# An edge layer on Trainium2: pair terms in four quarters of m times 32 channels

## The chip, the cores and the metric

One program runs on one core of one Trainium2 chip. The metric is the device time of an execution in microseconds. Three runs of the kernel before took 3580.55, 3586.84 and 3589.28 us; the median is 3586.84. Engines are named as in the profile: PE multiplies matrices (PEld loads its weights), DVE, ACT and POOL work elementwise, SP issues transfers. PSUM is the memory that PE writes its sums to, in eight banks of 512 f32 per partition; SBUF is the working memory.

## The reference

The input x is 4 samples of 56 x 56 pixels x 128 channels. Four layers follow one another, each with a group normalisation ahead and a residual sum behind. The change touches layer 1, the edge layer. In each sample and row l it forms, for every pair of pixels (n, m) of the row, a term of 128 channels, and sums over m:

```python
W1, W2 = (We[:, :f], We[:, f:])
proj_i = jnp.einsum('blnf,of->blno', x, W1)
proj_j = jnp.einsum('blnf,of->blno', x, W2)
edge = jax.nn.relu(proj_i[:, :, :, None, :] + proj_j[:, :, None, :, :] + be)
edge_sum = edge.sum(axis=3)
node_in = jnp.concatenate([x, edge_sum], axis=-1)
node = jax.nn.relu(jnp.einsum('blnc,oc->blno', node_in, Wn) + bn)
```

That is 4 x 56 x 56 x 56 x 128 pair terms. Layer 0 is a windowed attention with a global attention and an MLP, layer 2 a Fourier neural operator with attention over heads, layer 3 a convolution with sums.

## The kernel before

A sample lies as 128 channels (partitions) x 3136 pixels. For each of four samples, `first_layers` runs the attention (`fast_layer`) and then `edge_layer`; layer 2 and 3 follow for all samples. The change is in `edge_layer` (lines 1150 to 1256), `edge_weights` (1259) and the packing of weights in `l1_host` (1268). PE, ACT and DVE run the order of the program text there (a manual schedule); POOL has its own queue in program order.

The layer works in seven blocks of 8 image rows: 8 x 56 = 448 pixels, `NB`. For a block, `project` (line 1180) makes pc = W2 x and pa = W1 x in PSUM, one bank each. `evacuate` (1189) makes on ACT c = -(pc + be) in SBUF, a = pa as a copy in SBUF, and adds the bias bn to the residual. The relu of a pair term, relu(a - c), is max(a, c) - c, and it is made in two ways. A turn is four values of m, and EDGE_TURNS = "ddpddpdpddpddp" says who makes its tile of 128 channels x (4 m x 8 rows x 56 n) = 128 x 1792:

- nine turns "d": DVE writes max(pa, c) (line 1231, tile e_td, seven buffers). It reads pa straight from PSUM, and c from SBUF;
- five turns "p": POOL writes a - c from SBUF (1233, e_tp, four buffers), and ACT takes the relu in place (1235).

PE then sums the tile (1238): sixteen products per turn, each of a 32 x 32 identity with 32 channels x 448, for every pair of m (q) and channel quarter (r). Product (q, r) adds into partitions 32q to 32q + 31 of bank r of `acc`. So the four banks hold, for each quarter of channels, four partial sums over m. `acc` has one buffer of four banks; `mm` (pc, po and others) and `pa` have two banks each. These are all eight.

The max terms lack the sum of c over the m of the "d" turns. DVE makes it once a block (`rest`, line 1248). At the end of a block ACT copies all of acc, 128 x 1792, to SBUF (`e_sums`, 1250), and `output` (1200) forms po = Wn_x x - Wn_e rest + four products that add the quarters up, for the block before; then `project` is issued for the block two ahead. `finish` (1209) on DVE writes max(po, -bn) + (residual + bn), for the block two behind, after turn g = 3. `evacuate(j + 1)` stands after turn 5, the normalisation of block j + 2 after turn 8.

A product of f32 is two records in the profile. A name such as e_td is the tile, without its buffer's number.

Of the kernel before, what the change touches and what calls it, by code (L numbers as in the profile page):

```python
# [12 lines left out]
F32 = mybir.dt.float32  # L13
AF = mybir.ActivationFunctionType
ALU = mybir.AluOpType
AX = mybir.AxisListType
# [3 lines left out]
P = 128  # L20
B = 4
HH = 56
TOK = HH * HH
NB = 448
# [8 lines left out]
def bc(ap, axis, n):  # L33

    ap = ap.unsqueeze(axis)
    shape = list(ap.shape)
    shape[axis] = n
    return ap.to_broadcast(shape)


def blk(j):
    return slice(j * NB, (j + 1) * NB)
# [149 lines left out]
def apply_norm(k, out, xt, mr):  # L192
    k.nc.vector.tensor_scalar(out, xt, mr[:, 0:1], mr[:, 1:2], ALU.subtract, ALU.mult)
# [953 lines left out]
EDGE_TURNS = "ddpddpdpddpddp"  # L1147


def edge_layer(k, w, x1, st):  # L1150

    nc, tc = k.nc, k.tc
    xf = x1.rearrange("p l n -> p (l n)")
    nd = 4 * EDGE_TURNS.count("d")
    quarters = [slice(32 * q, 32 * q + 32) for q in range(4)]
    with ExitStack() as es:  # L1160
        big = es.enter_context(tc.tile_pool(name="e_big", bufs=1))
        wk = es.enter_context(tc.tile_pool(name="e_wk", bufs=2))
        psum = es.enter_context(tc.tile_pool(name="e_ps", bufs=2, space=PSUM))

        def bank():
            return psum.tile([P, 512], F32, tag="mm", name="e_mm")

        mr = group_norm_factors(k, wk, bank, st)
        xg = big.tile([P, TOK], F32, name="e_xg")
        shift = wk.tile([P, 1], F32, name="e_shift", bufs=1)  # L1170
        nc.vector.tensor_scalar(shift, mr[:, 0:1], mr[:, 1:2], -1.0, ALU.mult, ALU.mult)
        ready = {}

        def normed(j):
            if j < 2:
                apply_norm(k, xg[:, blk(j)], xf[:, blk(j)], mr)
            elif j < NBLK:
                nc.scalar.activation(xg[:, blk(j)], xf[:, blk(j)], AF.Identity, bias=shift, scale=mr[:, 1:2])

        def project(j):  # L1180
            if j >= NBLK:
                return
            pc = psum.tile([P, 512], F32, tag="mm", name="e_pc")
            nc.tensor.matmul(pc[:, :NB], w.W2, xg[:, blk(j)], start=True, stop=True)
            pa = psum.tile([P, 512], F32, tag="pa", name="e_pa")
            nc.tensor.matmul(pa[:, :NB], w.W1, xg[:, blk(j)], start=True, stop=True)
            ready[j] = pa, pc

        def evacuate(j):
            if j >= NBLK:  # L1190
                return
            pa, pc = ready[j]
            c = wk.tile([P, 8, HH], F32, name="e_c")
            nc.scalar.activation(c.rearrange("p l m -> p (l m)"), pc[:, :NB], AF.Identity, bias=w.nbe, scale=-1.0)
            a = wk.tile([P, NB], F32, name="e_a")
            nc.scalar.copy(a, pa[:, :NB])  # L1196
            nc.scalar.activation(xf[:, blk(j)], xf[:, blk(j)], AF.Identity, bias=w.bn)
            ready[j] = pa, a, c

        def output(j, rest, sums):  # L1200
            po = psum.tile([P, 512], F32, tag="mm", name="e_po")
            nc.tensor.matmul(po[:, :NB], w.Wn[:, 0, :], xg[:, blk(j)], start=True, stop=False)
            nc.tensor.matmul(po[:, :NB].rearrange("p (l n) -> p l n", l=8), w.nWn, bc(rest, 2, HH),
                             start=False, stop=False)
            for r in range(4):
                nc.tensor.matmul(po[:, :NB], w.Wnq[:, r, :], sums[:, r, :], start=False, stop=(r == 3))  # L1206
            return po

        def finish(j, po):

            nc.vector.scalar_tensor_tensor(xf[:, blk(j)], po[:, :NB], w.nbn, xf[:, blk(j)], ALU.max, ALU.add)

        with tc.manual_schedule(engines={mybir.EngineType.PE, mybir.EngineType.Activation, mybir.EngineType.DVE}):
            for j in range(2):
                normed(j)
            for j in range(2):
                project(j)
                evacuate(j)
            last = po = None
            for j in range(NBLK):  # L1220
                pa, a, c = ready.pop(j)
                acc = psum.tile([P, 4, 512], F32, name="e_acc", bufs=1)
                rest = wk.tile([P, 8], F32, name="e_rest")
                at = {"d": 0, "p": nd}
                for g, e in enumerate(EDGE_TURNS):
                    t = wk.tile([P, 4, 8, HH], F32, tag="e_" + e, name="e_t" + e, bufs=7 if e == "d" else 4)
                    cm = bc(c[:, :, at[e]:at[e] + 4].rearrange("p l m -> p m l"), 3, HH)
                    at[e] += 4
                    if e == "d":
                        am = bc(pa[:, :NB].rearrange("p (l n) -> p l n", l=8), 1, 4)  # L1230
                        nc.vector.tensor_tensor(t, am, cm, ALU.max)  # L1231
                    else:
                        nc.gpsimd.tensor_sub(t, bc(a.rearrange("p (l n) -> p l n", l=8), 1, 4), cm)  # L1233
                        tf = t.rearrange("p m l n -> p (m l n)")
                        nc.scalar.activation(tf, tf, AF.Relu)  # L1235
                    for q in range(4):
                        for r, o in enumerate(quarters):
                            nc.tensor.matmul(acc[quarters[q], r, :NB], k.ident[o, o],  # L1238
                                             t[o, q].rearrange("p l n -> p (l n)"),
                                             start=(g == 0), stop=(g == len(EDGE_TURNS) - 1))  # L1240
                    if g == 3 and po is not None:
                        finish(j - 2, po)
                    if g == 5 and j:
                        evacuate(j + 1)
                    if g == 8:
                        normed(j + 2)
                    if g == 9:
                        nc.vector.tensor_reduce(rest, c[:, :, 0:nd], AX.X, ALU.add)
                sums = wk.tile([P, 4, NB], F32, name="e_sums")
                nc.scalar.copy(sums, acc[:, :, :NB])  # L1250
                if last:
                    po = output(*last)
                project(j + 2)
                last = j, rest, sums
            finish(NBLK - 2, po)
            finish(NBLK - 1, output(*last))


def edge_weights(k, w, pool):

    for n, t in (("nbe", w.be), ("nbn", w.bn), ("nWn", w.Wn[:, 1, :])):
        r = pool.tile(list(t.shape), F32, name="e_" + n)
        k.nc.vector.tensor_scalar_mul(r, t, -1.0)
        setattr(w, n, r)


def l1_host(i):
    We, Wn = i["L1_conv_We"], i["L1_conv_Wn"]
    W2 = Wn[:, P:].T.reshape(4, 1, 32, P)
    return {  # L1270
        "w1_W1": We[:, :P].T, "w1_W2": We[:, P:].T, "w1_be": i["L1_conv_be"].reshape(P, 1),
        "w1_Wn": Wn.T.reshape(2, P, P).transpose(1, 0, 2), "w1_bn": i["L1_conv_bn"].reshape(P, 1),
        "w1_Wnq": np.broadcast_to(W2, (4, 4, 32, P)).reshape(4, P, P).transpose(1, 0, 2),
    }


# [1388 lines left out]
def group_norm_factors(k, pool, bank, st):  # L2665

    nc = k.nc
    mv = pool.tile([P, 2], F32, tag="mv", name="gf_mv")
    nc.vector.bn_aggr(mv, st.rearrange("p a b -> p (a b)"))
    ps = bank()  # L2670
    nc.tensor.matmul(ps[:, 0:1], k.g4, mv[:, 0:1], start=True, stop=True)
    mr = pool.tile([P, 2], F32, tag="mr", name="gf_mr")
    nc.vector.tensor_copy(mr[:, 0:1], ps[:, 0:1])
    t = pool.tile([P, 1], F32, tag="gt", name="gf_t")
    nc.vector.tensor_sub(t, mv[:, 0:1], mr[:, 0:1])
    nc.vector.tensor_mul(t, t, t)
    nc.vector.tensor_add(t, t, mv[:, 1:2])
    ps = bank()
    nc.tensor.matmul(ps[:, 0:1], k.g4, t, start=True, stop=True)
    nc.scalar.activation(t, ps[:, 0:1], AF.Sqrt, bias=k.eps)  # L2680
    nc.vector.reciprocal(mr[:, 1:2], t)
    return mr
# [158 lines left out]
```

## Time and profile before

| what | us |
|---|---|
| median of three runs | 3586.84 |
| the profiled execution, its own time | 3579.81 |
| its span in the profile | 3578.0 |
| PE busy in the span | 3372.0 (94%) |
| DVE busy | 2702.3 (76%) |
| ACT busy | 2089.9 (58%) |
| POOL busy | 1249.2 (35%) |
| first edge layer, 549.2 to 699.7: PE busy | 141.79 |
| the same: DVE, POOL, ACT busy | 130.02, 113.45, 83.44 |

The last two rows are the busy times of the engines in one stretch, and the other three edge layers (1211.3 to 1361.9, 1873.6 to 2024.9, 2540.2 to 2690.9) give nearly the same: DVE 130.1, 129.9 and 129.9, POOL 113.5, 113.5 and 113.7. Durations in the profile are from one execution. A group of instructions is written as line, engine, operation, output <- inputs, shapes, count; then the busy time and the mean nanoseconds of one; then the idle time of the engine just ahead of them and who ended it. PE's busy time says little by itself, since its matmuls overlap; the chain of waits says more.

### The profile page before, as it was taken

The numbers are of one execution on the slowest core, as the hardware profiler recorded it, in microseconds if no ns is written. First come the engines' busy times: TensorE is split into PE (matmuls) and PEld (weight loads), VectorE is DVE, ScalarE is ACT, GpSimd is POOL, SyncE is SP. The second block draws the span as 40 slices with busy tenths as digits, with TensorE's granted clock in tenths as the row PEclk, the third lists the DMA queues.
The fourth block names the chain that finished last, engine by engine and source line by source line (L and its number), as shares of the span: only waits on it lengthen the run. The fifth ranks groups of instructions, "written<-read, shape, count | busy, mean of one in ns | idle before, by whom it ended". The sixth has DMA issues, their size and how long they took to land.

```text
span 3578.0 us, 80873 instructions
## 1 busy us (share of the span) xinstructions
PE 3372.0 (94%) x36096; PEld 1549.4 (43%) x36096; DVE 2702.3 (76%) x2531; ACT 2089.9 (58%) x2103; POOL 1249.2 (35%) x752
## 2 busy tenths in 40 slices
PE   6999998989999898999999999999898899999998
PEld 4433344553333455333344643333456443336664
DVE  6588868767888696688859758887784678886776
ACT  4688865458888564688856458887552112214442
POOL 1000017600000581000018400000673778884686
PEclk8999999999999999999999999999998999999999
DMA  2144420014333000444310024442103027763101
GB/s 103 43 92 92 95 42 20 20 47 94 88 88 83 20 3 20 99 93 94 89 44 3 20 57 94 94 94 63 38 3 101 15 53 178 181 148 91 55 19 55
DMA packets 98076, 244.51 MB, mean 68 GB/s; under 512 B 64456, under 2 KB 69832, under 8 KB 92712
## 3 DMA queue, kind: packets, MB, share of 16 engines
q0 software_dynamic: 16128, 102.77, 14.2%
q1 hardware_dynamic: 74872, 123.64, 11.9%
q10 hardware_dynamic: 6720, 12.85, 1.3%
q8 instruction: 285, 4.67, 0.5%
q14 instruction: 71, 0.58, 0.1%
HBM read 79.46 MB, written 31.33 MB: 31 GB/s over the span
## 4 chain that ended last, share of the span: by engine, by line
PE 79%; DVE 10%; ACT 4%; issue 4%; POOL 3%; DMA 0%; POOLq 0%; DVEq 0%; ACTq 0%
PE f_pm L818 17%; PE f_pm L684 15%; PE u_po L1878 8%; PE e_acc L1238 7%; PE q_acc L1732 3%; DVE e_td L1231 3%; PE f_pm L791 2%; PE e_po L1206 2%; PE f_pm L770 2%; ACT f_ring L821 1%; PE f_pm L464 1%; PE o_d L2141 1%; DVE f_acc L673 1%; PE o_d L2538 1%; PE f_pm L715 1%
## 5 line engine op out<-in xcount | busy, mean ns | idle before, releaser
L821 ACT ACTIVATE f_ring<-f_pm 128x1792 f32<-128x1792 f32 (+1 forms) x764 | 1093.8, 1482 | 228.7 <-PE f_pm L818 181.2
L673 DVE TENSOR_TENSOR f_acc<-f_acc,f_ring 128x1792 f32<-128x1792 f32 x468 | 947.7, 2025 | 191.1 <-ACT f_ring L821 160.9
L818 PE MATMUL f_pm<-f_qT,f_kT 32*128 32x448 f32 x5376 | 725.2, 571 | 15.5 <-ACT f_ring L821 5.1
L684 PE MATMUL f_pm<-f_ring,f_va 128*32 128x448 f32 (+1 forms) x6304 | 589.4, 490 | 0.0
L663 POOL DMA_DIRECT2D f_far<-f_ring x112 | 96.6, 862 | 1329.3 <-ACT f_ring L821 1108.2
L1231 DVE TENSOR_TENSOR e_td<-e_pa,e_c 128x1792 f32<-128x1792 f32 x252 | 491.2, 2018 | 14.1 <-ACT e_a L1196 14.1
L1233 POOL TENSOR_TENSOR e_tp<-e_a,e_c 128x1792 f32<-128x1792 f32 x140 | 451.5, 3261 | 101.4 <-PE e_acc L1238 59.8
L818 PEld LDWEIGHTS f_pm<-f_qT,f_kT 32*128 32x128 f32 x5376 | 260.4, 183 | 417.2 <-ACT f_ring L821 304.7
L1238 PE MATMUL e_acc<-e_td,t_shared 32*32 32x448 f32 x8064 | 325.8, 545 | 24.9 <-DVE e_td L1231 24.0
L684 PEld LDWEIGHTS f_pm<-f_ring,f_va 128*32 128x32 f32 x6304 | 164.2, 109 | 409.7 <-issue 397.4
L1873 DVE TENSOR_TENSOR u_ud<-u_px,u_d 112x1792 f32<-112x1792 f32 x144 | 263.5, 1864 | 39.6 <-PE u_po L1878 35.4
L1235 ACT ACTIVATE e_tp<-e_tp 128x1792 f32<-128x1792 f32 x140 | 233.4, 1694 | 74.0 <-POOL e_tp L1233 74.0
L1875 POOL TENSOR_TENSOR u_up<-xh,u_d 112x1792 f32<-112x1792 f32 (+1 forms) x72 | 240.9, 3376 | 55.0 <-PE u_po L1878 39.7
L1238 PE MATMUL e_acc<-e_tp,t_shared 32*32 32x448 f32 x4480 | 222.6, 544 | 3.0 <-ACT e_tp L1235 2.4
L1878 PE MATMUL u_po<-u_ud,AT 112*64 112x448 f32 x1056 | 213.8, 544 | 1.9 <-DVE u_ud L1873 1.9
L1238 PEld LDWEIGHTS e_acc<-e_td,t_shared 32*32 32x32 f32 x8064 | 142.3, 103 | 138.4 <-DVE e_td L1231 79.4
L1878 PEld LDWEIGHTS u_po<-u_ud,AT 112*64 112x64 f32 x1056 | 74.4, 138 | 128.8 <-issue 112.9
L1250 ACT COPY e_sums<-e_acc 128x1792 f32<-128x1792 f32 x28 | 46.3, 1652 | 136.2 <-PE e_acc L1238 136.2
L1238 PEld LDWEIGHTS e_acc<-e_tp,t_shared 32*32 32x32 f32 x4480 | 96.5, 103 | 53.0 <-issue 16.6
L728 DVE RECIPROCAL f_den<-f_den 128x448 f32<-128x448 f32 x28 | 82.6, 2951 | 44.1 <-ACT f_den L725 44.1
L1717 POOL TENSOR_TENSOR q_u<-iS,q_g 128x1792 f32<-128x1792 f32 x32 | 102.8, 3236 | 23.0 <-PE q_acc L1732 22.8
L1732 PE MATMUL q_acc<-q_u,S 64*64 64x448 f32 x1024 | 104.6, 553 | 4.4 <-DVE q_u L1719 3.3
(525 smaller groups left out, 4511.6 us busy)
## 6 DMA issues: line engine op xcount, KB each, us to landing
f_far<-f_ring POOLq DMA_DIRECT2D x112, 896.0 KB, 6.3
u_d<-dd SPq DMA_DIRECT2D x46, 784.0 KB
f_far<-f_ring SPq DMA_DIRECT2D x28, 896.0 KB
xw<-in_x SPq DMA_DIRECT2D x4, 1568.0 KB
x2d<-x SPq DMA_DIRECT2D x4, 1568.0 KB
xat<-x SPq DMA_DIRECT2D x4, 1568.0 KB
x_xs<-xat ACTq DMA_DIRECT2D x32, 196.0 KB
xm<-x_ev ACTq DMA_DIRECT2D x64, 98.0 KB
```

Of the source, the lines that this page charges most:

```text
L673: nc.vector.tensor_add(e.acc, e.acc, slots(j, c))
L684: nc.tensor.matmul(e.po[heads[h], part], va[o, c, heads[h]], p, start=(c == 0), stop=(c == 23 and part.stop == NB))
L818: nc.tensor.matmul(ss[:, i, :NB], kT[heads[h], c * P:(c + 1) * P], qT[heads[h], blk(j)], start=True, stop=True)
L821: nc.scalar.activation(ring[:, slot:slot + m, :], ss[:, :m, :NB], AF.Exp, scale=scale)
L1231: nc.vector.tensor_tensor(t, am, cm, ALU.max)
L1233: nc.gpsimd.tensor_sub(t, bc(a.rearrange("p (l n) -> p l n", l=8), 1, 4), cm)
L1235: nc.scalar.activation(tf, tf, AF.Relu)
L1238: nc.tensor.matmul(acc[quarters[q], r, :NB], k.ident[o, o], t[o, q].rearrange("p l n -> p (l n)"), start=(g == 0), stop=(g == len(EDGE_TUR ...
L1732: nc.tensor.matmul(acc[bp][i][halves[hb % 2], hb // 2, :NB], x[o], u[o, 8 * hb:8 * hb + 8, :].rearrange("p h t -> p (h t)"), start=first, ...
L1873: nc.vector.tensor_mul(u, bc(px[:, :, :NB], 2, m), dm)
L1875: nc.gpsimd.tensor_mul(u, bc(x, 2, m), dm)
L1878: nc.tensor.matmul(po[64 * b2:64 * b2 + 64, :NB], st.AT[:, 8 * i + h0 + q, 2 * bp + b2, :], u[:, b2, q, :], start=(left == 16), stop=(left ...
```

## The change

The partitions of a pair term's tile are no longer 128 channels. They are four quarters of m times 32 channels, and a tile's first free dimension r is the quarter of the channels. A turn is still a tile of 128 x 1792 elements: one m of each quarter of 56 (M = 14 values a quarter, so 14 turns), for all four r.

- `project` makes pc in sixteen small products (128 x 32 weights, 112 columns), so that partitions 32q hold the m of quarter q; and pa in four products whose weights repeat 32 channels four times, into four banks (pa has one buffer of four banks).
- `evacuate` has two parts, after turns 5 and 7: c = -pc, and a in four pieces of 448 with the bias be. It is now a, in SBUF, that holds be.
- DVE's max and POOL's subtraction both read a and c from SBUF (`terms`).
- PE sums a turn with four products of 128 rows x 32 columns (S, four identities under one another), each into its 32 partitions of one bank. `acc` is one bank with two buffers. The sums of c are four more such products with -S.
- ACT's copy of the sums is 128 x 448, and `output` is two products in place of six.
- In the first block of a sample, the first two DVE tiles are made in pieces of 448, quarter by quarter. Turns of a kind "s" are provided for and don't occur in EDGE_TURNS, which is unchanged.
- `edge_weights` loses two of its three small instructions; `l1_host` packs the weights anew.

```diff
-    nd = 4 * EDGE_TURNS.count("d")
+    M = HH // 4
+    nd, ns = EDGE_TURNS.count("d"), EDGE_TURNS.count("s")
...
-            nc.tensor.matmul(pc[:, :NB], w.W2, xg[:, blk(j)], start=True, stop=True)
-            pa = psum.tile([P, 512], F32, tag="pa", name="e_pa")
-            nc.tensor.matmul(pa[:, :NB], w.W1, xg[:, blk(j)], start=True, stop=True)
-            ready[j] = pa, pc
+            xm = xg[:, blk(j)].rearrange("p (l m) -> p l m", l=8)
+            for r, o in enumerate(quarters):
+                for q in range(4):
+                    nc.tensor.matmul(pc[quarters[q], 8 * M * r:8 * M * (r + 1)].rearrange("p (l m) -> p l m", l=8),
+                                     w.W2[:, o], xm[:, :, M * q:M * (q + 1)], start=True, stop=True)
+            pa = psum.tile([P, 4, 512], F32, name="e_pa", bufs=1)
+            for r in range(4):
+                nc.tensor.matmul(pa[:, r, :NB], w.W1[:, r, :], xg[:, blk(j)], start=True, stop=True)
+            c = wk.tile([P, 4, 8, M], F32, name="e_c")
+            a = wk.tile([P, 4, NB], F32, name="e_a")
+            ready[j] = pc, pa, c, a
...
+            if part == 0:
+                nc.scalar.activation(c.rearrange("p r l m -> p (r l m)"), pc[:, :NB], AF.Identity, scale=-1.0)
+            for r in range(2 * part, 2 * part + 2):
+                nc.scalar.activation(a[:, r, :], pa[:, r, :NB], AF.Identity, bias=w.be[:, r:r + 1])
+            if part == 1:
+                nc.scalar.activation(xf[:, blk(j)], xf[:, blk(j)], AF.Identity, bias=w.bn)
+
+        def terms(j, m, t, r0, r1, e):
+            _, _, c, a = ready[j]
+            cm = bc(c[:, r0:r1, :, m], 3, HH)
+            am = a[:, r0:r1, :].rearrange("p r (l n) -> p r l n", l=8)
+            if e == "d":
+                nc.vector.tensor_tensor(t, am, cm, ALU.max)
+            else:
+                nc.gpsimd.tensor_sub(t, am, cm)
+                tf = t.rearrange("p r l n -> p (r l n)")
+                nc.scalar.activation(tf, tf, AF.Relu)
...
-            nc.tensor.matmul(po[:, :NB].rearrange("p (l n) -> p l n", l=8), w.nWn, bc(rest, 2, HH),
-                             start=False, stop=False)
-            for r in range(4):
-                nc.tensor.matmul(po[:, :NB], w.Wnq[:, r, :], sums[:, r, :], start=False, stop=(r == 3))
+            nc.tensor.matmul(po[:, :NB], w.Wn[:, 1, :], sums, start=False, stop=True)
...
-                acc = psum.tile([P, 4, 512], F32, name="e_acc", bufs=1)
-                rest = wk.tile([P, 8], F32, name="e_rest")
+                acc = psum.tile([P, 512], F32, name="e_acc")
+                rest = wk.tile([P, 4, 8], F32, name="e_rest")
...
+                early = {g: tile_of("d") for g in range(2)} if j == 0 else {}
+                for r in range(4 if early else 0):
+                    for g, t in early.items():
+                        terms(j, at["d"] + g, t[:, r:r + 1], r, r + 1, "d")
...
-                    if e == "d":
-                        am = bc(pa[:, :NB].rearrange("p (l n) -> p l n", l=8), 1, 4)
-                        nc.vector.tensor_tensor(t, am, cm, ALU.max)
...
-                        nc.gpsimd.tensor_sub(t, bc(a.rearrange("p (l n) -> p l n", l=8), 1, 4), cm)
...
-                    for q in range(4):
-                        for r, o in enumerate(quarters):
-                            nc.tensor.matmul(acc[quarters[q], r, :NB], k.ident[o, o],
-                                             t[o, q].rearrange("p l n -> p (l n)"),
-                                             start=(g == 0), stop=(g == len(EDGE_TURNS) - 1))
+                    for t, r0 in parts:
+                        for r in range(t.shape[1]):
+                            nc.tensor.matmul(acc[quarters[r0 + r], :NB], w.S[:, 0, :], t[:, r].rearrange("p l n -> p (l n)"),
+                                             start=(g == 0), stop=False)
...
-                    if g == 5 and j:
-                        evacuate(j + 1)
+                    if g == 5:
+                        evacuate(j + 1, 0)
+                    if g == 7:
+                        evacuate(j + 1, 1)
...
+                for r in range(4):
+                    nc.tensor.matmul(acc[quarters[r], :NB].rearrange("p (l n) -> p l n", l=8), w.S[:, 1, :],
+                                     bc(rest[:, r, :], 2, HH), start=False, stop=True)
+                sums = wk.tile([P, NB], F32, name="e_sums")
+                nc.scalar.copy(sums, acc[:, :NB])
...
+    W1 = np.broadcast_to(We[:, :P].T.reshape(P, 4, 1, 32), (P, 4, 4, 32)).reshape(P, 4, P)
+    S = np.tile(np.eye(32, dtype=np.float32), (4, 1))
```

More of the change, by code (lines that the diff above doesn't have):

```diff
@@ L1183, in project @@
             pc = psum.tile([P, 512], F32, tag="mm", name="e_pc")
-            nc.tensor.matmul(pc[:, :NB], w.W2, xg[:, blk(j)], start=True, stop=True)
-            pa = psum.tile([P, 512], F32, tag="pa", name="e_pa")
-            nc.tensor.matmul(pa[:, :NB], w.W1, xg[:, blk(j)], start=True, stop=True)
-            ready[j] = pa, pc
-        def evacuate(j):
+            xm = xg[:, blk(j)].rearrange("p (l m) -> p l m", l=8)
[3 more added lines that the diff above has]
+                                     w.W2[:, o], xm[:, :, M * q:M * (q + 1)], start=True, stop=True)
@@ L1190, in evacuate @@
+            pa = psum.tile([P, 4, 512], F32, name="e_pa", bufs=1)
[4 more added lines that the diff above has]
+            ready[j] = pc, pa, c, a
+        def evacuate(j, part):
             if j >= NBLK:
                 return
-            pa, pc = ready[j]
-            c = wk.tile([P, 8, HH], F32, name="e_c")
@@ L1194, in evacuate @@
[L1194 to L1200, printed above, removed]
+            pc, pa, c, a = ready[j]
+            if part == 0:
+                nc.scalar.activation(c.rearrange("p r l m -> p (r l m)"), pc[:, :NB], AF.Identity, scale=-1.0)
@@ L1201, in output, with tile_of @@
+        def tile_of(e, n=4):
+            return wk.tile([P, n, 8, HH], F32, tag="e_%s%d" % (e, n), name="e_t" + e,
+                           bufs=2 if n < 4 else 7 if e == "d" else 4)
+        def output(j, sums):
             po = psum.tile([P, 512], F32, tag="mm", name="e_po")
             nc.tensor.matmul(po[:, :NB], w.Wn[:, 0, :], xg[:, blk(j)], start=True, stop=False)
-            nc.tensor.matmul(po[:, :NB].rearrange("p (l n) -> p l n", l=8), w.nWn, bc(rest, 2, HH),
-                             start=False, stop=False)
@@ L1215, in edge_layer @@
                 normed(j)
-            for j in range(2):
-                project(j)
-                evacuate(j)
+            project(0)
+            for part in range(2):
+                evacuate(0, part)
+            project(1)
             last = po = None
             for j in range(NBLK):
-                pa, a, c = ready.pop(j)
-                acc = psum.tile([P, 4, 512], F32, name="e_acc", bufs=1)
-                rest = wk.tile([P, 8], F32, name="e_rest")
-                at = {"d": 0, "p": nd}
-                for g, e in enumerate(EDGE_TURNS):
-                    t = wk.tile([P, 4, 8, HH], F32, tag="e_" + e, name="e_t" + e, bufs=7 if e == "d" else 4)
-                    cm = bc(c[:, :, at[e]:at[e] + 4].rearrange("p l m -> p m l"), 3, HH)
-                    at[e] += 4
-                    if e == "d":
-                        am = bc(pa[:, :NB].rearrange("p (l n) -> p l n", l=8), 1, 4)
-                        nc.vector.tensor_tensor(t, am, cm, ALU.max)
-                    else:
-                        nc.gpsimd.tensor_sub(t, bc(a.rearrange("p (l n) -> p l n", l=8), 1, 4), cm)
-                        tf = t.rearrange("p m l n -> p (m l n)")
-                        nc.scalar.activation(tf, tf, AF.Relu)
-                    for q in range(4):
-                        for r, o in enumerate(quarters):
-                            nc.tensor.matmul(acc[quarters[q], r, :NB], k.ident[o, o],
-                                             t[o, q].rearrange("p l n -> p (l n)"),
-                                             start=(g == 0), stop=(g == len(EDGE_TURNS) - 1))
@@ new lines, in edge_layer @@
+                acc = psum.tile([P, 512], F32, name="e_acc")
+                rest = wk.tile([P, 4, 8], F32, name="e_rest")
+                at = {"d": 0, "p": nd + ns, "s": nd}
+                early = {g: tile_of("d") for g in range(2)} if j == 0 else {}
+                for r in range(4 if early else 0):
+                    for g, t in early.items():
+                        terms(j, at["d"] + g, t[:, r:r + 1], r, r + 1, "d")
+                for g, e in enumerate(EDGE_TURNS):
+                    m = at[e]
+                    at[e] += 1
+                    if g in early:
+                        parts = [(early[g], 0)]
+                    elif e == "s":
+                        parts = [(tile_of("d", 2), 0), (tile_of("p", 2), 2)]
+                        for t, r in parts:
+                            terms(j, m, t, r, r + 2, "p" if r else "d")
+                    else:
+                        parts = [(tile_of(e), 0)]
+                        terms(j, m, parts[0][0], 0, 4, e)
+                    for t, r0 in parts:
+                        for r in range(t.shape[1]):
+                            nc.tensor.matmul(acc[quarters[r0 + r], :NB], w.S[:, 0, :], t[:, r].rearrange("p l n -> p (l n)"),
+                                             start=(g == 0), stop=False)
@@ L1241, in edge_layer @@
                     if g == 3 and po is not None:
                         finish(j - 2, po)
-                    if g == 5 and j:
-                        evacuate(j + 1)
-                    if g == 8:
[L1246 to L1250, printed above, removed]
+                    if g == 5:
+                        evacuate(j + 1, 0)
@@ new lines, in edge_layer @@
+                    if g == 7:
+                        evacuate(j + 1, 1)
+                    if g == 10:
+                        normed(j + 2)
+                    if g == 8:
+                        if ns:
+                            nc.vector.tensor_reduce(rest[:, 0:2], ready[j][2][:, 0:2, :, 0:nd + 1], AX.X, ALU.add)
+                        nc.vector.tensor_reduce(rest[:, 2 if ns else 0:4], ready[j][2][:, 2 if ns else 0:4, :, 0:nd], AX.X, ALU.add)
+                for r in range(4):
+                    nc.tensor.matmul(acc[quarters[r], :NB].rearrange("p (l n) -> p l n", l=8), w.S[:, 1, :],
+                                     bc(rest[:, r, :], 2, HH), start=False, stop=True)
@@ L1253, in edge_layer @@
                 project(j + 2)
-                last = j, rest, sums
+                last = j, sums
             finish(NBLK - 2, po)
@@ L1259, in edge_weights @@
 def edge_weights(k, w, pool):
[L1261 to L1264, printed above, removed]
+    w.nbn = pool.tile([P, 1], F32, name="e_nbn")
+    k.nc.vector.tensor_scalar_mul(w.nbn, w.bn, -1.0)
 def l1_host(i):
     We, Wn = i["L1_conv_We"], i["L1_conv_Wn"]
-    W2 = Wn[:, P:].T.reshape(4, 1, 32, P)
+    W1 = np.broadcast_to(We[:, :P].T.reshape(P, 4, 1, 32), (P, 4, 4, 32)).reshape(P, 4, P)
+    S = np.tile(np.eye(32, dtype=np.float32), (4, 1))
     return {
-        "w1_W1": We[:, :P].T, "w1_W2": We[:, P:].T, "w1_be": i["L1_conv_be"].reshape(P, 1),
+        "w1_W1": W1, "w1_W2": We[:, P:].T, "w1_be": np.tile(i["L1_conv_be"].reshape(4, 32).T, (4, 1)),
         "w1_Wn": Wn.T.reshape(2, P, P).transpose(1, 0, 2), "w1_bn": i["L1_conv_bn"].reshape(P, 1),
-        "w1_Wnq": np.broadcast_to(W2, (4, 4, 32, P)).reshape(4, P, P).transpose(1, 0, 2),
+        "w1_S": np.stack((S, -S), 1),
     }
```

## The prediction

> **What bounds the kernel now.** I read the page's groups first, to find the lines that the change touches, then the chain of waits in order of time over one edge layer, then the timeline of VectorE (DVE) and GpSimd (POOL), because both will read the same operands afterwards. The three groups of the layer, from the page:
>
> ```profile
> L1231 DVE TENSOR_TENSOR e_td<-e_pa,e_c 128x1792 f32<-128x1792 f32 x252 | 491.2, 2018 | 14.1 <-ACT e_a L1196 14.1
> L1233 POOL TENSOR_TENSOR e_tp<-e_a,e_c 128x1792 f32<-128x1792 f32 x140 | 451.5, 3261 | 101.4 <-PE e_acc L1238 59.8
> ...
> L1238 PE MATMUL e_acc<-e_td,t_shared 32*32 32x448 f32 x8064 | 325.8, 545 | 24.9 <-DVE e_td L1231 24.0
> ```
>
> And the chain in order of time through two middle blocks of the first sample (start, length, what):
>
> ```profile
> 612.79 3.01 PE e_po L1206 x8
> 617.30 13.47 PE e_acc L1238 x436
> 632.48 3.01 PE e_po L1206 x8
> 636.98 13.47 PE e_acc L1238 x435
> ```
>
> A block takes 632.48 - 612.79 = 19.69 us, and PE never rests in it: 14 turns at 13.47 / 14 = 0.962 us, then twelve passes of the output product and four of the projection at 3.01 / 8 = 0.376 us, 6.0 us. DVE needs 9 x 1.94 (nine e_td in a row take 17.46 us in the timeline) + about 0.36 + 0.60 for the reduction and the finish = 18.4, POOL 5 x 3.23 = 16.1 (five in a row take 16.13). So **PE bounds the layer by about 1 us a block, and DVE and POOL are both close behind it, running side by side.** One sample's layer goes from its first e_td at 553.64 us to the end of its last finish at 699.71: 146.1 us, four times.
>
> **What the change does to PE.** A turn becomes 4 products of 128 rows x 32 columns x 448 in place of 16 of 32 x 32. Their shape is in the page, in the attention:
>
> ```profile
> L673 DVE TENSOR_TENSOR f_acc<-f_acc,f_ring 128x1792 f32<-128x1792 f32 x468 | 947.7, 2025 | 191.1 <-ACT f_ring L821 160.9
> ...
> L684 PE MATMUL f_pm<-f_ring,f_va 128*32 128x448 f32 (+1 forms) x6304 | 589.4, 490 | 0.0
> ```
>
> L684: 589.4 us / 6304 records = 93.5 ns; a product is two records, so a turn is 8 x 93.5 = 0.75 us and 14 turns 10.5. The sums of c cost one more such group, 0.75. The output product falls from 12 passes to 4 (1.5 us), the projection grows from 4 passes to 8 (3.0) plus 32 small records of 112 columns: between 32 x 23.4 ns (a quarter of 93.5 each) = 0.75 us and 32 x 93.5 = 3.0; I take 1.2, near the pace of 30 ns of the 32 x 32 records now. Sum 17.0 us a block, bounds 16.5 to 18.8, against 19.5. Two banks for the sums also let a block begin before the copy of the last one ends. **Taken alone this would hand the bound to DVE, at 18.4.**
>
> ACT: three more evictions of 448 (0.63 each), the copy of sums falls from 1.65 to about 0.55: 83.4 us busy of 150 now, some 89 afterwards. No bound. The weights are loaded in one pack before; two small DVE instructions at the start go.
>
> **What it does to DVE, and this decides.** Before, e_td reads pa in PSUM and c in SBUF. Afterwards a and c both lie in SBUF, for DVE and for POOL. By itself that costs nothing: L673 above has both inputs in SBUF and takes 2025 ns, against 2018. [...]
>
> But L673 runs where POOL computes nothing. I looked for DVE instructions with two SBUF inputs that meet a computing POOL. Three places show the same thing. First DVE, then POOL, in the softmax of the scores (start, length, engine, line, out<-in):
>
> ```profile
> 2857.87 1.09 DVE L1758 TENSOR_TENSOR y<-y,q_red 128x896 f32<-128x896 f32 x1
> ...
> 2860.28 2.68 DVE L1766 TENSOR_TENSOR y<-y,q_den 128x896 f32<-128x896 f32 x1
> ...
> 2866.21 1.09 DVE L1766 TENSOR_TENSOR y<-y,q_den 128x896 f32<-128x896 f32 x1
> ```
> ```profile
> 2854.29 7.72 POOL L1717 TENSOR_TENSOR q_u<-iS,q_g 128x1792 f32<-128x1792 f32 x2 [1.98 <-PE q_acc L1732]
> ```
>
> L1766 alone takes 1.09 us. The one at 2860.28 took 2.68 and ended at 2862.96, 0.95 us after POOL's pair ended (2854.29 + 7.72 = 2862.01), and 896 elements at DVE's pace (0.93 us) is just that: it stood until POOL had finished, then ran. The other way round, POOL's two took 7.72 where the line's median is 3.19: 1.3 us more, about the part of the two L1758 that lay over them; the second, at 4.09 us the line's longest, began 0.05 us after L1758 had, so it waited 0.89 us for it. Meanwhile the one-SBUF-input e_td keeps 2014 to 2027 ns in all 252 cases, most of them beside a busy POOL.
>
> ```profile
> 541.75 0.91 POOL L804 TENSOR_TENSOR x<-xf,xw 128x343 f32<-128x343 f32 x1 [3.95 <-DVE xf L793]
> 542.62 0.58 POOL L805 TENSOR_TENSOR x<-xf,xw 128x28 f32<-128x28 f32 x1
> ```
> ```profile
> 541.04 0.63 DVE L793 SCALAR_TENSOR_TENSOR xf<-f_pm,t_first,xf 128x392 f32<-128x392 f32 x1 [4.17 <-PE f_pm L791]
> ...
> 542.06 1.02 DVE L799 SCALAR_TENSOR_TENSOR xf<-xf,t_first,xw 128x392 f32<-128x392 f32 x1
> ```
>
> The upper fence is POOL, the lower DVE in the same two microseconds, at the end of the first layer. The same instruction on 392 elements takes 0.63 us with one input in PSUM and 1.02 with both in SBUF beside POOL, in all four samples; L805 behind it is held in turn (0.58, median 0.25). And in the longest case one element waited 5.46 us, over a dozen of POOL's instructions that followed one another without a gap:
>
> ```profile
> 2723.54 5.46 DVE L1458 TENSOR_TENSOR s_t<-s_mv,s_mr 128x1 f32<-128x1 f32 x1
> ```
>
> **So a DVE instruction with two SBUF inputs and a POOL instruction that reads SBUF do not run side by side; one waits for the whole of the other.** [...]
>
> **The sum.** After the change each block's nine e_td and five e_tp stand in one line. If each runs in one piece: 17.46 + 16.13, less 0.14 us at each change of owner (L1766 began its wait with that much already behind it: 1.09 - 0.95; POOL's 4.09 likewise): 33.3 us. If POOL's five come singly: after POOL a DVE instruction needs 1.87 + 0.015, after DVE a POOL one 3.26 - 0.14: 5 x (1.88 + 3.12) + 4 x 1.94 = 32.8. I take 33.1. The reduction and the finish read one SBUF tensor (their rows L1248 and L1211 do not stretch beside POOL) and hide in POOL's turn. PE's 17 us and ACT's hide too. Does the line ever stand empty? Seven buffers of e_td and four of e_tp mean that when one engine has no buffer left, PE is waiting for the other's tile, so I put nothing on it, with the bound below. For one sample:
>
> - Start: pa now needs 8 passes, at the slow start (1.59 us for two at 551.45), but e_td begins with the first quarter: first e_td at about 553.6 as now. Eight pieces of 448 for two instructions: 8 x 0.54 - 3.9 = 0.4. All of a is there for POOL only about 3 us later, beside DVE's pieces: 1 us put down for holes.
> - Seven blocks: 7 x 33.1 = 231.7.
> - End: last Relu 1.69, two groups of products 1.5, the copy beside the first of two outputs of 1.5 each, finish 0.68, hand-overs 0.3: 7 (now 12.2, from the last e_td's end at 687.52 to 699.71).
>
> 240.1 against 146.1, +94 us a sample, +376 in four: **3579.8 + 376 = 3956.** 3579.81 is the profiled execution's own time (span 3578.0 and 1.8 around it); the runs' median of 3586.84 lies 7 us above it and I keep 3956, inside that difference. A measurement here can tell about 0.3%, 11 us, from no change.
>
> Bounds: 9 x 1.867 + 5 x 3.05 = 32.0 a block if every edge hides, -31 us. Upwards 0.2 us at each of ten changes of owner is +56; PE, now idle half the time, may be granted a slower clock, which shows only in the tails, up to +12. That gives 3925 to 4024, widened below for a lock that is let go a little early.
>
> **Rivals.**
> - *The engines wait on each other too.* finish(j-2) stands in DVE's queue ahead of six e_td; it waits for po, that is for the last Relu, PE and the output: 1.69 + 0.75 + 0.75 + 1.5 = 4.7 us. If POOL has then filled its buffers, the line is empty: 28 x 4.7 = +132, 4088. Against: POOL can go on for two tiles (6.5 us) in that time. 8%.
> - *Shared by element, not by instruction.* 14 x 1.867 = 26.1 us a block, +45 a sample, 3760. Against: the 0.89 us wait is nearly a whole instruction. 6%.
> - *Faster.* [...] 5%.
> - That the change isn't in effect is excluded: the order of instructions shows e_td<-e_a,e_c on DVE, 35 e_tp a sample on POOL, four products a turn.
> - The forecast itself: 80%; 1% for no change.
>
> **What would show it.** Mean e_td or e_tp, or both, stretched well beyond 2.02 and 3.26, with DVE and POOL rows that together fill a block of about 33 us; PE at some 50% of the layer, waiting for e_td and e_tp; products of 93.5 ns. Wrong if e_td keeps 2.02 while POOL runs (faster), or if DVE and POOL both stand idle in the middle of blocks (slower yet). Faster 0.05, within 0.3% 0.01, slower 0.94.

## The result, and the profile after

The changed kernel takes 3964.39 us (median of four runs, 3955.64 to 3970.18) against 3585.96 (3580.55 to 3589.28): the ratio is 1.106, with an interval of 1.104 to 1.108. The forecast was 3956, with bounds worked out as 3925 to 4024 and widened below. The profiled execution took 3970.18 us, its span 3968.4.

The lines of its page that answer to those shown of before, costliest first (line, engine, operation, tiles, shapes, count, then busy time and mean ns of one, then the idle time ahead):

```profile
L1216 DVE TENSOR_TENSOR e_td<-e_a,e_c 128x1792 f32<-128x1792 f32 (+1 forms) x276 | 909.7, 3358 | 25.9 <-ACT e_a L1206 25.9
...
L1218 POOL TENSOR_TENSOR e_tp<-e_a,e_c 128x1792 f32<-128x1792 f32 x140 | 603.0, 4325 | 334.5 <-PE e_acc L1266 270.8
L1266 PE MATMUL e_acc<-e_td,t_edge 128*32 128x448 f32 x2016 | 308.8, 679 | 335.2 <-DVE e_td L1216 334.3
```

DVE's max has gone from 491.2 us busy to 909.7, with the same elements and the same operation. POOL's subtraction has gone from 451.5 to 603.0. PE, which never rested in the middle blocks, now stands idle for 334.3 us ahead of tiles that DVE makes.

The chain that ended last, in order of time, through the same blocks of the first sample (start, length, what):

```profile
649.27 14.62 DVE e_td L1216 x3
663.93 3.22 PE e_acc L1266 x16
...
671.28 3.20 PE e_pa L1194 x8
674.48 3.19 PE e_acc L1266 x32
...
678.48 3.65 issue
...
682.57 14.63 DVE e_td L1216 x3
```

Three e_td take 14.6 us there. Three that no POOL instruction meets take 5.88 (at 782.41). The minimum, median and maximum of the two lines tell why, since a waiting instruction counts as running:

```profile
L1216 DVE TENSOR_TENSOR e_td<-e_a,e_c x276: 615/3669/5080, 555.9 to 3065.1; 128x1792 f32<-128x1792 f32 x122, 128x448 f32<-128x448 f32 x16
```
```profile
L1218 POOL TENSOR_TENSOR e_tp<-e_a,e_c x140: 3252/4657/5152, 557.6 to 3051.9; 128x1792 f32<-128x1792 f32 x140
```

The longest of both is near 5.1 us, which is one of the other's plus its own: 3.2 + 1.9. A short e_td of 448 elements, 0.62 us alone, takes 3.67 (the median above) when it meets POOL. So each waits for at most one whole instruction of the other, and they take turns.

The busy times of the engines in six blocks, from reduction to reduction (586.32 to 782.05):

```profile
core 0: us, PE busy (x) PEld busy (x) DVE busy (x) ACT busy (x) POOL busy (x), PEclk, DMA share, GB/s
586.32:782.05 195.73, 127.77 (x940) 37.96 (x940) 195.73 (x67) 69.91 (x70) 127.58 (x29) 0.80 0.00 1
```

195.73 / 6 = 32.6 us a block, where it was 19.7; DVE is at work or waiting in its own instruction in every microsecond of it. The six blocks hold 54 e_td but 29 e_tp, not 30, because POOL had made one tile ahead in the first block. With the thirtieth, at 3.1 us, a block would be 33.1 us, an estimate.

### The profile page after: what moved, and what is told of

Its sections match the earlier page's. It is cut to its first block, busy times and chain, and to the rows that moved or that the text cites. A ratio compares the mean times of both kernels' runs of the same rounds, so it can differ in the third digit from the quotient of the medians.

```text
span 3968.4 us, 64164 instructions
## 1 busy us (share of the span) xinstructions
PE 3453.6 (87%) x27696; PEld 1447.0 (36%) x27696; DVE 3112.0 (78%) x2553; ACT 2099.5 (53%) x2187; POOL 1400.2 (35%) x752
## 4 chain that ended last, share of the span: by engine, by line
PE 65%; DVE 21%; issue 8%; ACT 4%; POOL 2%; DMA 0%; DVEq 0%; POOLq 0%; ACTq 0%; SPq 0%
PE f_pm L818 16%; DVE e_td L1216 14%; PE f_pm L684 14%; PE u_po L1911 7%; PE q_acc L1765 3%; PE e_acc L1266 2%; PE f_pm L791 2%; PE f_pm L770 2%; ACT f_ring L821 1%; PE o_d L2571 1%; PE e_pa L1194 1%; PE s_pr L1560 1%; PE f_pm L464 1%; PE o_d L2174 1%; DVE f_acc L673 1%
## 5 line engine op out<-in xcount | busy, mean ns | idle before, releaser
L1216 DVE TENSOR_TENSOR e_td<-e_a,e_c 128x1792 f32<-128x1792 f32 (+1 forms) x276 | 909.7, 3358 | 25.9 <-ACT e_a L1206 25.9
L1218 POOL TENSOR_TENSOR e_tp<-e_a,e_c 128x1792 f32<-128x1792 f32 x140 | 603.0, 4325 | 334.5 <-PE e_acc L1266 270.8
L1266 PE MATMUL e_acc<-e_td,t_edge 128*32 128x448 f32 x2016 | 308.8, 679 | 335.2 <-DVE e_td L1216 334.3
L1284 ACT COPY e_sums<-e_acc 128x448 f32<-128x448 f32 x28 | 14.9, 532 | 500.0 <-PE e_acc L1281 500.0
L1266 PEld LDWEIGHTS e_acc<-e_td,t_edge 128*32 128x32 f32 x2016 | 57.1, 123 | 556.2 <-DVE e_td L1216 497.0
L1266 PE MATMUL e_acc<-e_tp,t_edge 128*32 128x448 f32 x1120 | 179.5, 696 | 0.0
L793 DVE SCALAR_TENSOR_TENSOR xf<-f_pm,t_first,xf 128x392 f32<-128x392 f32 x28 | 17.5, 626 | 113.3 <-PE f_pm L791 113.3
```

The source lines that it names most:

```text
L1218: nc.gpsimd.tensor_sub(t, am, cm)
L1266: nc.tensor.matmul(acc[quarters[r0 + r], :NB], w.S[:, 0, :], t[:, r].rearrange("p l n -> p (l n)"), start=(g == 0), stop=False)
```

## Experiments

Two theories stood against each other. **The operand:** e_td with both inputs in SBUF and POOL's e_tp exclude each other, and nothing else of the change costs anything. **The layout:** the time goes to PE's new products, the four-bank pa, the pieces of evacuation, or to an SBUF operand that is slow by itself.

### One operand, in the old layout

```diff
-                        am = bc(pa[:, :NB].rearrange("p (l n) -> p l n", l=8), 1, 4)
+                        am = bc(a.rearrange("p (l n) -> p l n", l=8), 1, 4)
```

> The kernel before, with one edit: DVE's max reads a from its SBUF copy and no longer from PSUM; layout, products and everything else as before. Theory (a DVE instruction with two SBUF inputs and a POOL instruction that reads SBUF exclude each other): 9 e_td and 5 e_tp stand in one line, 33 us a block in place of 19.7, about +97 us a sample, some 3970 us. Rival (the new layout costs the time: PE's 128 x 32 products, the four-bank pa, the pieces of evacuation): about 3586, e_td at 2.02 us.

It took 3977.72 us (one run; before it 3584.32 on the same chip). Its groups of DVE and POOL:

```profile
L1231 DVE TENSOR_TENSOR e_td<-e_a,e_c 128x1792 f32<-128x1792 f32 x252 | 911.8, 3679 | 14.1 <-ACT e_a L1196 14.1
...
L1233 POOL TENSOR_TENSOR e_tp<-e_a,e_c 128x1792 f32<-128x1792 f32 x140 | 644.6, 4622 | 282.6 <-PE e_acc L1238 238.7 <-issue 41.5 <-ACT e_tp L1235 1.9
```

911.8 us busy against 909.7 in the changed kernel: the old layout with this one edit loses as much as the whole change. The layout is not needed for the loss.

### POOL writes only

```diff
-                nc.gpsimd.tensor_sub(t, am, cm)
+                nc.gpsimd.memset(t, 0.0)
```

> The changed kernel, with POOL's subtraction replaced by a memset of the same tile (the subtraction is left out, so the p turns add nothing): POOL writes SBUF and reads none. Theory (it is the reading that excludes): e_td 2.02 us throughout, DVE bounds a block at 18.5 us, about 3545 us. Rival 1 (any POOL instruction on SBUF excludes it): 9 x 1.94 + 5 x 1.5 = 25 us a block, about 3735. Rival 2 (the layout or the SBUF operand itself costs the time): near 3960, e_td still above 3 us.

It took 3548.36 us (one run; its sums lack the p turns). The two groups:

```profile
L1216 DVE TENSOR_TENSOR e_td<-e_a,e_c 128x1792 f32<-128x1792 f32 x244 | 475.9, 2009 | 0.0
```
```profile
L1218 POOL MEMSET e_tp<- 128x1792 f32 x140 | 222.2, 1601 | 300.9 <-PE e_acc L1266 294.9 <-PE f_pm L791 6.0
```

e_td keeps its 2.01 us beside POOL's memsets, and a memset its 1.60. Writing excludes nothing here.

### POOL reads one input

```diff
-                nc.gpsimd.tensor_sub(t, am, cm)
+                nc.gpsimd.tensor_copy(t, am)
```

> The changed kernel, with POOL's subtraction a - c replaced by a copy of a (c is left out of the p turns): POOL reads one SBUF input in place of two, where the run with a memset read none. Theory (any reading of SBUF by POOL excludes an e_td with two SBUF inputs): e_td stretched again, a block of 9 x 1.88 to 1.94 and five of POOL's instructions at their own length, which no run shows yet, between 1.6 us (memset) and 3.26 (subtraction): 25 to 33 us a block, 3740 to 3960 us. Rival (only POOL's instructions with two SBUF inputs exclude it): e_td 2.02 us, about 3548.

It took 3740.90 us (one run; its p turns lack c), at the lower end of what was expected.

```profile
L1216 DVE TENSOR_TENSOR e_td<-e_a,e_c 128x1792 f32<-128x1792 f32 x244 | 650.0, 2724 | 0.0
```
```profile
L1218 POOL COPY e_tp<-e_a 128x1792 f32<-128x1792 f32 x140 | 369.3, 2649 | 348.8 <-PE e_acc L1266 288.2 <-ACT e_a L1206 59.3 <-ACT e_tp L1220 1.3
```

One input is enough. The shortest copies between 610 and 660 us take 1.88 us, a memset 1.60, yet the mean copy is 2.65 and the mean e_td 2.72. From the first e_td to the last it is 177.1 us in the first sample, 25.3 a block, against 232.4 and 33.2 in the changed kernel. So what POOL's instruction costs DVE is its length, not the number of its inputs.

### All turns on DVE

```diff
-EDGE_TURNS = "ddpddpdpddpddp"
+EDGE_TURNS = "dddddddddddddd"
```

> The changed kernel with all 14 turns on DVE and none on POOL. Theory: with nobody to wait for, e_td takes 2.02 us each; 14 x 1.94 + 0.96 for the reduction and the finish = 28.1 us a block, 205 us a sample in place of 241: about 3825 us, faster than the changed kernel although DVE does half as much again. Rival (an e_td with both inputs in SBUF is slow by itself, 3.36 us as its mean now): 14 x 3.3 = 46 us a block, about 4320.

It took 3820.05 us (one run).

```profile
L1216 DVE TENSOR_TENSOR e_td<-e_a,e_c 128x1792 f32<-128x1792 f32 x384 | 746.8, 2008 | 0.0
```

Both inputs lie in SBUF, and without POOL e_td takes 2.01 us. DVE does 14 turns in place of 9, and the kernel is 144 us faster than the changed one: with that operand, POOL's five turns cost more than they take off DVE. From the first e_td to the last it is 196.8 us, 28.1 a block, as expected.

### c in PSUM

```diff
             pc, _, c, a = ready[j]
+            if e == "d":
+                c = pc[:, :NB].rearrange("p (r l m) -> p r l m", r=4, l=8)
...
-                nc.scalar.activation(c.rearrange("p r l m -> p (r l m)"), pc[:, :NB], AF.Identity, scale=-1.0)
+                nc.scalar.copy(c.rearrange("p r l m -> p (r l m)"), pc[:, :NB])
...
-            pc = psum.tile([P, 512], F32, tag="mm", name="e_pc")
+            pc = psum.tile([P, 512], F32, name="e_pc")
...
+    w.nW2 = pool.tile([P, P], F32, name="e_nW2")
+    k.nc.vector.tensor_scalar_mul(w.nW2, w.W2, -1.0)
```

`project` uses nW2; po and acc have bufs=1.

> The changed kernel, in which DVE's max reads c from PSUM (the projection's own bank, made with negated weights) and a from SBUF; POOL still reads the SBUF copies. pc gets two banks of its own, po and the sums one each. Everything else of the new layout stays. Theory: no instruction excludes another any more, e_td 2.02 us, DVE bounds a block at 18.5 us and PE needs 17: 135 us a sample from the first e_td, about 3545 us, faster than both kernels. Rival (the new layout has another limit, PE's slower clock or the single banks): 3586 or above.

It took 3557.68 us (four runs, 3555.86 to 3561.97), a ratio of 0.993 to the kernel before, interval 0.991 to 0.995. The rival said 3586 or above.

```profile
L1218 DVE TENSOR_TENSOR e_td<-e_a,e_pc 128x1792 f32<-128x1792 f32 x244 | 474.8, 2003 | 0.0
...
L1220 POOL TENSOR_TENSOR e_tp<-e_a,e_c 128x1792 f32<-128x1792 f32 x140 | 451.7, 3266 | 87.2 <-ACT e_a L1206 60.6 <-PE e_acc L1268 26.2
```
```profile
586.63:678.29 91.66, 85.55 (x800) 30.50 (x792) 91.66 (x56) 60.77 (x63) 84.89 (x27) 1.00 0.01 1
```

Five blocks from reduction to reduction (PE, PEld, DVE, ACT, POOL busy, then PE's granted clock) take 91.66 us, 18.3 each: DVE bounds them, POOL keeps its 3.27 us and runs side by side. PE is busy for 85.55 / 5 = 17.1. This kernel has everything of the changed one but the second SBUF input and the second buffers of po and the sums, and beats both. It missed the expected 3545 by 13 us. From the first e_td to the last finish a sample took 135.1 us, as expected, although its end was longer than I had put (7.5 us from the last e_td to the last finish, not 6). But the first e_td came 6.9 to 8.3 us after the normalisation, where I had put 4.4: some 12 us in four samples. And from the last finish of the last edge layer to the end of the span it took 900.4 us, against 887.2 in the kernel before; no run tried why.

### The start of a sample

The first e_td waits for ACT's first piece of a. In the changed kernel ACT took it at 555.26, only after the last pass of pa (551.34 + 3.89 = 555.23), though it needs the first bank alone:

```profile
551.47 0.54 ACT L1204 ACTIVATE e_c<-e_pc 128x448 f32<-128x448 f32 x1 [2.71 <-PE e_pc L1190]
555.26 2.21 ACT L1206 ACTIVATE e_a<-e_pa,t_edge 128x448 f32<-128x448 f32 x4 [3.25 <-PE e_pa L1194]
```

The edit, on top of c in PSUM:

```diff
-            pa = psum.tile([P, 4, 512], F32, name="e_pa", bufs=1)
+            pa = [psum.tile([P, 512], F32, tag="pa%d" % r, name="e_pa", bufs=1) for r in range(4)]
```

> The kernel with c in PSUM, and pa as four tiles of one bank in place of one tile of four. In the changed kernel ACT took the first quarter of a only after the last of pa's eight passes had ended (3.9 us after the first began), so the first e_td came at 555.9 us and not at 553.6. Theory: that wait belongs to the tile; with four tiles the first e_td comes about 2 us earlier in each sample, 8 us in all, about 3550. Rival: ACT's wait is for PE's queue whatever the tile, 3558.

It took 3548.43 us (3546.45 to 3550.34), a ratio of 0.990 to the kernel before, interval 0.989 to 0.992, and is the fastest of the kernels that compute the whole layer.

```profile
555.70 0.53 ACT L1204 COPY e_c<-e_pc 128x448 f32<-128x448 f32 x1 [2.60 <-PE e_pc L1190]
557.48 0.63 ACT L1206 ACTIVATE e_a<-e_pa,t_edge 128x448 f32<-128x448 f32 x1 [1.25 <-PE e_pa L1194]
558.37 2.14 ACT L1206 ACTIVATE e_a<-e_pa,t_edge 128x448 f32<-128x448 f32 x3 [0.25 <-PE e_pa L1194]
```

The wait ahead of the first piece fell from 3.3 us to 1.25, and from the normalisation to the first e_td it is 4.7 us in place of 6.9 to 8.3. The wait belonged to the tile: ACT now starts on the first piece at 557.48, and the pieces behind it wait for pa once more (0.25 us), so the first did not wait for the last bank.

### Half a turn moved to POOL

```diff
-EDGE_TURNS = "ddpddpdpddpddp"
+EDGE_TURNS = "ddpdpdsdpddpdp"
```

> The kernel with c in PSUM, and half a turn moved from DVE to POOL: the turns are ddpdpdsdpddpdp, s being half DVE's and half POOL's. Theory (DVE bounds a block at 18.3 us, PE follows at 17.0, POOL at 16.1): DVE 8.5 x 1.94 + 1.2 = 17.7, POOL 5.5 x 3.23 = 17.8, so 17.9 us a block, 0.4 less, 28 times: about 3546. Rival (PE or ACT bounds already, or the shorter pieces cost what they spare): 3558 or above.

It took 3558.26 us (3553.96 to 3559.17; ratio 0.993, 0.991 to 0.994), no gain. Five blocks of it and the start of POOL's work:

```profile
584.17:675.38 91.21, 87.23 (x814) 30.65 (x810) 87.63 (x62) 68.54 (x71) 91.21 (x31) 1.00 0.00 1
```
```profile
557.95 124.52 POOL L1220 TENSOR_TENSOR e_tp<-e_a,e_c 128x1792 f32<-128x1792 f32 x42 [14.56 <-ACT e_a L1206]
```

POOL is busy in every microsecond now and DVE is not: the bound has passed over. POOL's pace of 124.52 / 7 = 17.8 us a block is what was expected. (The five blocks shown are those of DVE, 18.2 us each; in the first of them DVE loses the lead that it had.) But POOL starts 1.7 us after DVE, and the sample then ends with POOL's last tile, ACT's relu and PE: 9.3 us from the last e_td to the last finish, where it was 7.5. What the blocks gave, the ends took back. With the four tiles of pa as well:

> Both edits of the two runs before together. Theory: the start of a sample and the pace of its blocks are separate, the gains add: about 3538. Rival: the moved half turn makes POOL the bound, whose start the four tiles do not hasten as much: 3546.

3554.00 us (3544.34 to 3555.17; ratio 0.991, 0.989 to 0.992). The gains did not add; its interval overlaps that of the four tiles alone, and the median is not better.

```profile
558.53 124.54 POOL L1220 TENSOR_TENSOR e_tp<-e_a,e_c 128x1792 f32<-128x1792 f32 x42 [13.64 <-issue]
```

POOL again runs without a pause, and now starts 2.8 us after DVE's first tile (555.70) in place of 1.7: the four tiles hasten DVE, while POOL is the bound. That is the rival's mechanism, but its 3546 is missed as well, by 8 us.

## Why the prediction was right

**The mechanism.** The step that decided, that a DVE instruction with two SBUF inputs and a POOL instruction that reads SBUF stand in one line, is shown by five runs: it comes with the one operand in the old layout, goes when POOL only writes, comes back when POOL reads one input, is not there without POOL, and goes when c moves to PSUM.

**The sum, term by term.** A block: 33.1 forecast, 32.6 measured between reductions, 33.1 with the tile that POOL had made ahead. The end of a sample: 7, measured 6.45 (before 12.2). The sum of the four layers, from the first normalisation to the last finish, went from 603.0 to 983.5 us, +380.5, against +376. The profiled executions differ by 390.4, and the medians by 378.4. Of the 9.9 us that the layers leave of the 390.4, 7.7 lie behind the last edge layer (894.9 us from its last finish to the end of the span, against 887.2). The sum had no term for them. In the old layout with the one operand changed that stretch takes 886.8 us, so it does not come with the wait; what makes it longer stays open.

**The start was mis-sized.** "First e_td at about 553.6 as now": it came at 555.93, and in the other samples 2.4 to 4 us later than before too. I had let e_td begin with the first quarter; ACT waited for all of pa, and the run with four tiles shows that the tile was the reason. It is worth some 12 us in four samples. In the total it is half hidden: from the first e_td to the last finish a sample took 238.0 to 238.9 us against 240.1 worked out, 6.5 us less in four.

**PE was mis-sized, and it did not matter.** "Products of 93.5 ns": they took (308.8 + 179.5) / 3136 = 156 ns of busy time. PE came to 65% of the blocks, not 50%. The 93.5 itself came from a row that mixes two sizes:

```profile
L684 PE MATMUL f_pm<-f_ring,f_va 128*32 128x448 f32 x4448 | 494.9, 545 | 0.0
...
L684 PE MATMUL f_pm<-f_ring,f_va 128*32 128x224 f32 x1856 | 133.3, 359 | 0.0
```

The products of 448 columns alone come to 494.9 / 4448 = 111 ns. That 93.5 is near the pace in a stream is luck: where the clock was 1.00 in the changed kernel, a turn that stands alone took 0.96 us (at 682.26) and two in a row 1.71 (at 674.41), so the second costs 0.75. Two things stretch PE in the changed kernel. Turns often arrive alone, at 0.96 us or more. And the granted clock was 0.80 in those blocks, against 1.00 with c in PSUM: in the chain above 16 records took 3.22 us at 663.93, where the clock was 0.50, and 32 took 3.19 at 674.48, where it was 1.00. All of that lay behind DVE and POOL. With c in PSUM a block of PE measured 17.1 us busy, against 17.0 worked out.

**"Does the line ever stand empty?"** Hardly. DVE's 195.73 us of 195.73 do not show it, since DVE also works on the reduction and the finish. I had let both hide in POOL's turn. In four of the six blocks the finish did not: POOL was waiting for a buffer then. First DVE, then POOL:

```profile
649.19 23.55 DVE L1216 TENSOR_TENSOR e_td<-e_a,e_c 128x1792 f32<-128x1792 f32 x6
672.67 0.67 DVE L1234 SCALAR_TENSOR_TENSOR x<-e_po,e_nbn,x 128x448 f32<-128x448 f32 x1
673.26 8.94 DVE L1216 TENSOR_TENSOR e_td<-e_a,e_c 128x1792 f32<-128x1792 f32 x3
```
```profile
667.33 3.53 POOL L1218 TENSOR_TENSOR e_tp<-e_a,e_c 128x1792 f32<-128x1792 f32 x1 [5.33 <-PE e_acc L1266]
677.05 13.26 POOL L1218 TENSOR_TENSOR e_tp<-e_a,e_c 128x1792 f32<-128x1792 f32 x3 [6.19 <-PE e_acc L1266]
```

Between 672.74 and 673.26 neither an e_td nor an e_tp runs. Such gaps come to 2.1 us of the 195.73. The rival in which finish(j-2) stalls the line is out: DVE's idle time ahead of the finish (L1234) is 20.3 us in all, at the ends of samples. The rival of sharing by element is out by the maxima of 5.1 us, whole instructions. Faster would have shown as an e_td of 2.02 us beside POOL; the mean of a whole e_td was 3.52.

**The wait of 5.46 us** of one element (L1458 before) lay beside ten of POOL's instructions. In the changed kernel the two took turns after every instruction, even where the next of the same engine was ready. What made that one case different wasn't tried and stays open; the sum needed only that nothing overlaps, and that held.

**The SBUF operand by itself** costs and spares next to nothing: 2008 ns with both in SBUF and no POOL, 2018 with a in PSUM, 2003 with c in PSUM.

**Two terms of the range.** No run shows a lock that is let go early; what the runs showed in its place is that an instruction waits for at most one whole instruction of the other engine (5.08 and 5.15 us at the longest). Nor does a run show the 12 us put down for a slower clock of PE: the granted clock was 0.80 in the six blocks of the changed kernel, and the end of a sample still took 6.45 us where 7 was put.

## What to carry to other kernels

Before an operand moves from PSUM to SBUF, look who else reads SBUF at that time: here DVE and POOL shared the work of a stage and POOL's instructions read SBUF, and with both tensor inputs of DVE's instruction in SBUF the two engines' times added (33 us a block, in place of 18.3 with one of them in PSUM). Such a wait hides inside the durations, so compare one line's minimum with its mean (2.005 and 3.68 us in the old layout with that one operand changed); an engine that is busy all the time may be waiting, as DVE was in 195.73 us of 195.73. And when the cause of a loss is a single operand, undo that alone: here the rest of the change was a gain of 0.7%, and of 1% with pa in four tiles.

## What the runs showed of the hardware

- In the changed kernel waiting engines took turns strictly: with both ready, no e_td waited for more than one e_tp (longest 5.08 us = 3.2 + 1.9) and no e_tp for more than one e_td (5.15).
- POOL's copy with one SBUF input excluded e_td just as its subtraction with two did (mean of a whole e_td 2.72 and 3.52 us); its memset didn't (2.01).
- Where PE waited for DVE, its granted clock was lower: 0.80 in the changed kernel's blocks (PE busy 65%), 1.00 with c in PSUM (93%). That the waiting lowers it was not tried by itself.
